# The last unit of a two-batch attention block: three query tiles taken together in wide pieces, the fourth tile's keys moved to the end

## The chip, the core and the metric

The kernel runs on one core of one Trainium2 chip, as one launch. The metric is device time in microseconds (us) of one execution. Three executions of the kernel before took 610.93, 608.96 and 611.11 us, so the median is 610.93. The engines are called by the profile's names: PE is TensorE (matrix products, transposes), PEld its weight load, DVE VectorE, ACT ScalarE, POOL GpSimd, SP SyncE, whose queue starts the DMAs.

## The reference, cut to what matters

Two batches of 1024 tokens with 512 channels pass one gated attention block in float32, with 32 heads of 16 channels:

```python
xn = layernorm(x)
q, k, v = xn @ Wq.T + bq, xn @ Wk.T + bk, xn @ Wv.T + bv      # (2, 32, 1024, 16) after the split in heads
scores = einsum('bhqd,bhkd->bhqk', q, k) / sqrt(16)
scores = where(tril(ones(l, l)), scores, -inf)                # causal
s = (softmax(scores) @ v) @ Wo.T + bo
result = xn @ W_base.T + b_base
logits = xn @ W_gate.T                                        # 8 experts, two are kept
delta = einsum('bner,eor->bno', (xn @ A) * route_w, B)        # rank 16 each
return x + s * silu(result + delta)
```

The change touches the attention of the last unit (below) and the output projection of the last 512 tokens.

## The kernel before, in words

**Units and steps.** Attention is done in 16 units `(b, oc, c)`: a batch, a group of 8 heads (`oc`, 0 to 3) and a chunk of 512 queries (`c`, 0 or 1). A unit is a row of steps. A step has at most 512 columns of work for each of its four head slots: a list of pieces `(par, kt, q0, w, col)`, each of them the `w` queries from `q0` of the chunk against one tile of 128 keys, `kt`, for the heads of one parity, laid at column `col`. A unit with `c = 0` has 5 steps, one with `c = 1` has 13; in all there are 144, numbered 0 to 143. The last unit is `(1, 3, 1)`, steps 131 to 143. They are called step 1 to step 13 of the last unit here.

For step `n` the main loop (at the end of `direct`) issues, in this order: `scores(n)`, which is 4 matmuls for each piece (line 1375) into two PSUM tiles `s`, and two exponentials on ACT over 128 x 1024 (line 1384); `values(n - 1)`, which is 4 matmuls for each piece of the step before (line 1420) into an accumulator `av` for each parity; `masked(n)`, which multiplies diagonal pieces with a triangular mask on DVE; and `fill(n)`, in which all other work is placed. Each engine works through its instructions in the order of issue. The two `s` tiles of a step have two buffers in all, so `scores(n + 1)` can begin only when the exponentials of step `n` have read them.

**The last unit before.** Every other unit uses pieces up to 512 wide. The last one (`last_steps`, line 1075) goes query tile by query tile: for each of the 4 tiles of 128 queries, for both parities, first the diagonal key tile and then all earlier ones, each piece 128 wide, four pieces to a step. Tile 0 is complete after step 3, tile 1 after step 6, tile 2 after step 9 and tile 3 after step 13. When a tile is complete, DVE copies its sums out of `av` (`avs`), PE transposes them (`pt_o`, line 936, one transpose for each parity), DVE takes reciprocals of the denominators and multiplies (`rc_last`, `olast`), PE transposes the result (`pt_y`, line 966), and ACT copies that to `oT` (line 967). Only then can the tile's output projection `po` run (`whole_task`, 4 blocks of matmuls) and the two DVE operations and the DMA of the output (`finish_tile`) follow. For tile 3 the first three blocks of `po` are done ahead (`most_task`), and one block is left for the end (`rest_task`). All of `pt_o`, `pt_y`, `po` and the products `p`, `q` of other tasks take turns in two PSUM buffers (tag `mm`).

**The planner in `fill`.** Other PE work (projections, gates, output projections) is cut into blocks of 16 matmuls, `MM` = 0.853 in the planner's units. In each step `fill` computes a share, and issues blocks while what is spent, plus half a block, is less than the share. The share is the larger of two rates. The first is even: before step `begin` (136, that is `len(plan) - 8`) it brings what is left down to `last_work` (16 blocks and 4 transposes) by that step; from there on it spreads what is left over the steps that remain. The second is a due rate: for each task that is due at a step still to come, all work left up to and with that task, divided by the steps until then. The task `out_task` for batch 1, chunk 0 (14 blocks) is due at step 137; `whole_task` of tiles 0 and 1 at 143; `most_task` at 144. `whole_task` of tile 2 is held to step 143. A list `late` holds the `pt_o` and `pt_y` work, taken out at the end of a `fill`, one or two entries in each step (`post_tile` two steps after its values, `turn_last` in the `fill` after the task that asks for it).

Of the kernel before, what the change touches and what calls it, by code (L numbers as in the profile page):

```python
# [17 lines left out]
P = 128  # L18
# [7 lines left out]
KC = D // P  # L26
# [54 lines left out]
def direct(ctx, tc, sound, x, wq, wk, wv, wo, wb, wa, wg, wB, bq, bk, bv, bo, bb, out):  # L81
# [121 lines left out]
    rc_last = cst.tile([P, 2, TT, 4], F32, name="rc_last")  # L203

    MM = 0.853
    TR = 0.11

# [721 lines left out]
        later.append((n + 4 + wait, collect))  # L929
        later.append((n + 6 + wait, finish))  # L930

    def post_tile(b, oc, c, t, pars, avs):

        pt2 = mm_tile("pt_o")[:, 0 : 2 * P].rearrange("p (a s r) -> p a s r", a=2, s=4)
        for a in pars:
            nc.tensor.transpose(
                pt2[:, a].rearrange("p s r -> p (s r)"), avs[:, a * P : a * P + P], ident
            )
# [4 lines left out]
        for a in pars:  # L943
# [9 lines left out]
    posts, posted, later, patient, last_out = {}, [], [], [], []  # L953

    def project_out(po, b, c, t, k0, k1):
        for k in range(k0, k1):
# [4 lines left out]
            if k < k1 - 1:  # L961
                yield

    def turn_last(b, c, t, turned):
        pt = mm_tile("pt_y")[:, 0:P]
        nc.tensor.transpose(pt, last_out[0][:, t], ident)
        nc.scalar.copy(oTs[b, c][:, KC - 1, t * P : t * P + P], pt)
        turned.append(t)
# [26 lines left out]

    def whole_task(b, c, t, hold=0):

        turned = []
        yield lambda: turn_last(b, c, t, turned), TR
        while not turned or normalized(b, c) < KC - 1:  # L1000
            yield WAIT
        while now[0] < hold:
            yield WAIT
        po = mm_tile("po")
        for _ in project_out(po, b, c, t, 0, KC):
            yield MM
        finish_tile(b, c, t, po)
        yield MM
# [10 lines left out]

    def rest_task(b, c, t):  # L1020

        turned = []
        list(last_in_range())
        yield lambda: turn_last(b, c, t, turned), TR
        while not turned:
# [12 lines left out]
        yield MM  # L1038
# [35 lines left out]

    def last_steps(c):

        k0 = c * TT
        pieces = []
        for t in range(TT):
            for par in range(2):  # L1080
                for kt in [k0 + t] + list(range(k0 + t)):
                    pieces.append((par, kt, t * P, P, len(pieces) % 4 * P))
        return [pieces[n : n + 4] for n in range(0, len(pieces), 4)]

    units = [(b, oc, c) for b in range(NB) for oc in range(KC) for c in range(NC)]

# [79 lines left out]
    for b in range(NB):  # L1166
        for c in range(NC):
# [61 lines left out]
                lambda u=(b, c, "h"): now[0] > turned_at.get(u, now[0]) + 2,  # L1229
            )  # L1230
            if (b, c) != (NB - 1, NC - 1):
                by = min(len(plan) - 3, done + (21 if c else 19 if b else 30))
                stage(
                    out_task, ("out", b, c), by, 14 * MM, {"x": 1}, [("g", b, c)],
                    lambda b=b, c=c: normalized(b, c) == KC and (b, c) in g_tiles, {"x": 1},
                )
            else:
                before = starts[b, KC - 1, c] + 2
                Task(len(plan) - 9, bases_task(b, c), 0.0, after=before - 12, takes={"xnT": 2})
                n = len(units) - 3  # L1240
                Task(len(plan) - 12, test_task(0, n, 0), 0.0, after=before - 10)
                Task(
                    len(plan) - 1, test_task(n, n + 2, 1), 0.0, after=before,
                    ready=lambda: sum(len(x) for x in posts.values()) == len(units) - 1,
                )
                for t in range(TT - 1):

                    last_but_one = t == TT - 2
                    Task(
                        len(plan) + 9 if last_but_one else len(plan) - 1,  # L1250
                        whole_task(b, c, t, len(plan) - 1 if last_but_one else 0),
                        4 * MM + TR, after=before, ready=lambda t=t: posted.count(t) == 2,
                    )
# [4 lines left out]
                Task(  # L1258
                    len(plan) + 1, rest_task(b, c, TT - 1), MM + TR, after=before,
                    ready=lambda: posted.count(TT - 1) == 2,  # L1260
                )

# [3 lines left out]
        task.due = staged[k].due - int(staged[k].cost / 1.7) + 1 if k else -9  # L1266
    tasks.sort(key=lambda x: x.due)
    total = sum(x.cost for x in tasks)
    last_work = 16 * MM + 4 * TR
    spent = 0.0  # L1270
    late, active = [], []
    SV = 2.08
# [25 lines left out]
    def fill(n):  # L1298
# [4 lines left out]
        within = 0 <= n < len(plan)  # L1303
        for x in tasks:
            x.waiting = False

        begin = len(plan) - 8
        even = (total - spent) / max(1, len(plan) - n)
        if n == len(plan) - 1:
            even = 2 * MM  # L1310
# [8 lines left out]
        while True:  # L1319
            free = [x for x in tasks if x.cost and x.released(n)]  # L1320
            if not free or free[0].due > n + 1:
                due = [x.steps.__name__ for x in tasks if x.cost and x.due <= n + 1]
                if due:
                    assert late, (n, due)
                    turn_late()
                    continue
                if not free or spent + MM / 2 >= share:
                    break
            task = active[0] if active else free[0]
            active[:] = [task]  # L1330
            ve.ready = clock[0] + SV + spent - begun_at + MM
            cost = task.step()
            if cost is None or cost is WAIT:
                task.waiting = True
                active.clear()
            elif isinstance(cost, tuple):
                late.append((n, cost[0]))
                spent += cost[1]
            else:
                spent += cost  # L1340
        ve.ready = 0.0
# [22 lines left out]
    avs_now, avs_last = {}, {}  # L1364

    def scores(n):
        (b, oc, c), pieces, _, _ = plan[n]
# [38 lines left out]
    def values(n, pt):  # L1406
        (b, oc, c), pieces, is_first, is_last = plan[n]
        if is_first:
            avs_now.clear()
        for par, kt, q0, w, col in pieces:  # L1410
# [4 lines left out]
            if (b, oc, c) == units[-1]:  # L1415
                start = kt * P == c * C + q0
                stop = kt * P == c * C + q0 - P
            for s in range(4):
                h = 8 * oc + 2 * s + par
                nc.tensor.matmul(  # L1420
                    avs_now[par][32 * s : 32 * s + 32, q0 : q0 + w],
                    lhsT=vs[b, kt][:, h * VS - HD * par : h * VS - HD * par + HP],
                    rhs=pt[:, s, col : col + w],
                    start=start,
                    stop=stop,
                )
        ve.ready = clock[0] + 2.0
        if (b, oc, c) == units[-1]:
            for par, kt, q0, _, _ in pieces:
                t = q0 // P  # L1430
                if kt * P != c * C + q0 - P or not (par or t == TT - 1):
                    continue

                pars = [par] if t == TT - 1 else [0, 1]
                if t not in avs_last:
                    avs_last[t] = sb.tile([P, C], F32, tag="avs", name="avs")
                avs = avs_last[t]
                for p in pars:
                    ve.tensor_copy(avs[:, p * P : p * P + P], avs_now[p][:, q0 : q0 + P])
                late.append((n + 2, lambda a=(b, oc, c, t, pars, avs): post_tile(*a)))  # L1440
# [21 lines left out]
    third = next(x for x in tasks if x.begun)  # L1462
    third.step()
    turn_late()
    while late or tasks:
        fill(last + 99)


# [460 lines left out]
```

## Time and profile before

The profiled execution took 610.35 us, 0.58 below the median of the three; its span from first to last instruction is 608.5 us. The rest of 1.85 us lies outside the span.

| | |
|---|---|
| PE busy | 591.7 us, 97% of the span |
| ACT busy | 319.1 us, 52% |
| DVE busy | 392.1 us, 64% |
| last unit, first scores to the last `pn` | 545.45 to 601.26 us |
| from there to the end of the span | 7.2 us |

The last unit on PE, by step, from the order of its instructions in time (a block is 16 matmuls of 128 x 256, or 8 of 128 x 512):

| step | scores begin | blocks of other work | first or second transposes |
|---|---|---|---|
| 1, 2, 3 | 545.45, 549.28, 553.13 | 2, 2, 2 | |
| 4 | 556.97 | 1 | |
| 5 | 559.94 | 2 | `pt_o` of tile 0 |
| 6 | 564.36 | 0 | `pt_y` of tile 0 |
| 7 | 567.35 | 2 | |
| 8 | 571.44 | 2 | `pt_o` of tile 1 |
| 9 | 575.64 | 2 | `pt_y` of tile 1 |
| 10 | 579.73 | 3 | |
| 11 | 584.42 | 2 | `pt_o` of tile 2 |
| 12 | 588.62 | 0 | `pt_y` of tile 2 |
| 13 | 591.00 | 2, then 3 more | `pt_o`, `pt_o`, `pt_y` of tile 3 |

Lines of the timeline give the start, the time, the engine and line, the operation with what it writes and reads, the shapes, how many instructions were merged, and in brackets the idle time before them with what ended it. A PE line's time overlaps with the next line's by about 0.1 us, because matmuls are pipelined; so differences of starts are used. Where PE waits inside a group of merged matmuls, the group's time is longer and no bracket is shown.

### The profile page before, as it was taken

To read this page: it belongs to the slowest core of one execution; us is meant where nothing else is said; L and a number is where in the kernel's file an instruction comes from. 1 tells how busy PE (TensorE), PEld (TensorE's weight loads), DVE (VectorE), ACT (ScalarE), POOL (GpSimd) and SP (SyncE) were. 2 spreads that over 40 slices of the span, in tenths; PEclk is the share of its full clock that TensorE was granted. 3 is DMA by queue.
4 is the path that set the end of the run, shared out by engine and by line. 5 is a ranking of instruction groups with operands and counts; after the bars stand their busy time and mean duration, and the time that the engine had idled before them with its cause. 6 is when DMAs were issued, how large, how long until landed. Compare 5 with 4: busy or idle time off the path is not lost.

```text
span 608.5 us, 19376 instructions
## 1 busy us (share of the span) xinstructions
PE 591.7 (97%) x8615; PEld 290.6 (48%) x8615; DVE 392.1 (64%) x831; ACT 319.1 (52%) x368; POOL 9.2 (2%) x26
## 2 busy tenths in 40 slices
PE   8999999899999999999999999999999999999994
PEld 8335344444445544444345544454445444457651
DVE  4546786476479857475588656766359755697632
ACT  2435445455565655556555555556654555565441
POOL 2000000000001000000000000000000000000000
PEclk9999999899999999999999999999999999999998
DMA  8513476223300643424043321630112013402101
GB/s 262 138 67 129 136 247 213 107 90 89 88 3 5 185 154 94 119 91 142 18 125 89 111 90 39 186 114 4 37 54 89 24 41 116 149 20 75 48 28 40
DMA packets 57931, 58.69 MB, mean 96 GB/s; under 512 B 8312, under 2 KB 49280, under 8 KB 57456
## 3 DMA queue, kind: packets, MB, share of 16 engines
q1 hardware_dynamic: 57824, 57.38, 30.6%
q8 instruction: 69, 1.13, 0.8%
q14 instruction: 22, 0.18, 0.1%
q10 hardware_dynamic: 16, 0.00, 0.0%
HBM read 43.24 MB, written 14.12 MB: 94 GB/s over the span
## 4 chain that ended last, share of the span: by engine, by line
PE 86%; DVE 6%; DMA 4%; ACT 2%; SPq 1%; issue 1%; DVEq 0%
PE s L1375 23%; PE av L1420 21%; PE p L221 19%; PE q L221 11%; PE po L221 2%; PE pv L221 2%; PE ph L221 2%; ACT pt L1384 2%; DMA kept<-wqk 1%; PE pk L221 1%; PE pq L221 1%; DMA w_out<-in_wo_dram 1%; DMA x<-in_x_dram 1%; DMA dens<-den 1%; DVE pt L55 1%
## 5 line engine op out<-in xcount | busy, mean ns | idle before, releaser
L1384 ACT ACTIVATE pt<-s 128x1024 f32<-128x1024 f32 x288 | 279.1, 1021 | 237.9 <-PE s L1375 237.9
L1375 PE MATMUL s<-qT,kT 32*128 32x512 f32 (+3 forms) x1824 | 166.8, 465 | 0.4 <-ACT pt L1384 0.3
L1420 PE MATMUL av<-pt,v 128*32 128x512 f32 (+3 forms) x1824 | 154.9, 443 | 0.8 <-DVE pt L55 0.8
L55 DVE TENSOR_TENSOR pt<-pt,causal 128x512 f32<-128x512 f32 (+1 forms) x166 | 91.1, 566 | 78.9 <-ACT pt L1384 78.5
L1375 PEld LDWEIGHTS s<-qT,kT 32*128 32x128 f32 x1824 | 73.7, 185 | 66.8 <-issue 47.5
L1420 PEld LDWEIGHTS av<-pt,v 128*32 128x32 f32 x1824 | 44.0, 109 | 89.8 <-issue 58.4
L221 PE MATMUL p<-wt,asum 128*32 128x256 f32 x960 | 58.4, 379 | 0.0
L221 PE MATMUL q<-asum,wqk 128*32 128x256 f32 x832 | 50.9, 379 | 0.2 <-DVE qT L55 0.2
L221 PEld LDWEIGHTS p<-wt,asum 128*32 128x32 f32 x960 | 32.1, 110 | 26.2 <-issue 10.0
L221 PE MATMUL q<-xnT,wqk 128*32 128x256 f32 x624 | 40.0, 383 | 4.4 <-DVE kT L55 3.9
L221 PEld LDWEIGHTS q<-asum,wqk 128*32 128x32 f32 x832 | 27.6, 110 | 23.2 <-issue 7.2
L221 PEld LDWEIGHTS q<-xnT,wqk 128*32 128x32 f32 x624 | 20.4, 110 | 25.6 <-issue 10.5
L55 DVE TENSOR_TENSOR g<-p,g 128x512 f32<-128x512 f32 x28 | 18.9, 688 | 20.5 <-PE p L221 20.4
L221 PE MATMUL p<-w,xnT 128*32 128x256 f32 x448 | 27.3, 379 | 0.0
L55 DVE SCALAR_TENSOR_TENSOR kT<-q,kT 128x256 f32<-128x256 f32 x39 | 16.4, 422 | 16.1 <-PE q L221 15.0
L55 DVE TENSOR_TENSOR v<-p,v 128x512 f32<-128x512 f32 x21 | 14.1, 686 | 12.4 <-PE p L221 12.3
L221 PE MATMUL p<-w,asum 128*32 128x256 f32 x320 | 20.3, 379 | 0.0
L221 PEld LDWEIGHTS p<-w,xnT 128*32 128x32 f32 x448 | 14.4, 110 | 11.7 <-issue 3.9
L55 DVE TENSOR_TENSOR x<-p,x 128x512 f32<-128x512 f32 x21 | 14.2, 686 | 8.6 <-PE p L221 8.6
L748 ACT ACTIVATE sg<-g 128x512 f32<-128x512 f32 x16 | 10.1, 630 | 17.6 <-DVE g L55 17.6
L708 ACT ACTIVATE qT<-qT,half 128x512 f32<-128x512 f32 x26 | 18.8, 722 | 0.4
L221 PEld LDWEIGHTS ph<-wag_sb,xnT 128*32 128x32 f32 x512 | 15.8, 113 | 6.4 <-issue 4.9
(132 smaller groups left out, 484.1 us busy)
## 6 DMA issues: line engine op xcount, KB each, us to landing
wt<-kept SPq DMA_DIRECT2D x40, 256.0 KB
x<-in_x_dram SPq DMA_DIRECT2D x16, 256.0 KB
scr<-sq SPq DMA_DIRECT2D x6, 512.0 KB
xnT<-scr SPq DMA_DIRECT2D x24, 128.0 KB
w<-in_wb_dram SPq DMA_DIRECT2D x12, 256.0 KB
xr<-in_x_dram SPq DMA_DIRECT2D x12, 256.0 KB
out_dram<-x SPq DMA_DIRECT2D x12, 256.0 KB
w<-in_wv_dram SPq DMA_DIRECT2D x9, 256.0 KB
```

What stands on the lines that cost most here:

```text
L55: return getattr(self.engine, name)(*args, **named)
L221: nc.tensor.matmul(o[j : j + 32], lhsT=lhsT[:, j : j + 32] if len(lhsT.shape) == 2 else lhsT[:, j // 32], rhs=rhs, start=start, stop=stop,)
L708: nc.scalar.activation(qT[:, par], qT[:, 0], AF.Copy, scale=half[:, par : par + 1])
L748: nc.scalar.activation(sg, g(i, j), AF.Tanh, scale=0.5)
L1375: nc.tensor.matmul(ss[s // 2][:, s % 2, col : col + w], lhsT=kT[rows, kt % TT * P : kt % TT * P + P], rhs=qTs[b, oc, c][rows, par, q0 : q0 ...
L1384: nc.scalar.activation(pt[:, 2 * pair : 2 * pair + 2], ss[pair], AF.Exp, scale=0.25)
L1420: nc.tensor.matmul(avs_now[par][32 * s : 32 * s + 32, q0 : q0 + w], lhsT=vs[b, kt][:, h * VS - HD * par : h * VS - HD * par + HP], rhs=pt[ ...
```

## The change

- `last_steps`: steps 1 to 9 of the last unit now take tiles 0 to 2 (384 queries) together. Steps 1 to 3 have parity 0, steps 4 to 6 parity 1, with key tiles 0 to 2 in pieces 384 wide, beside which key tile 3 stands in pieces 128 wide. Steps 7 and 8 have key tiles 4 and 6, step 9 key tile 5 of both parities. Steps 10 to 13 have tile 3 in pieces of 128, parity 0 first. So tiles 0, 1 and 2 are complete together after step 9, tile 3 after step 13 as before. There are 13 steps as before; steps 1 to 9 have two pieces in place of four.
- `values`: the sums of tiles 0 to 2 are copied by one DVE copy of 384 columns for each parity; three `post_tile` calls are put into `late` for step 10 (one step after the values, before two). Tile 3 is as before.
- `fill`: in the last unit up to three entries of `late` are taken at the end of a step.
- `turn_last` is no longer asked for by `whole_task` or `rest_task`: `post_tile` puts it on a list `turns` for the next step, and `fill` issues it ahead of its other work.
- Numbers of the planner: `begin` is `len(plan) - 3` (141), `last_work` is 13 blocks, the transposes (`TR`) have no cost, `out_task` of batch 1, chunk 0 is due at 140.

```diff
-        for t in range(TT):
-            for par in range(2):
-                for kt in [k0 + t] + list(range(k0 + t)):
-                    pieces.append((par, kt, t * P, P, len(pieces) % 4 * P))
-        return [pieces[n : n + 4] for n in range(0, len(pieces), 4)]
+        for par in range(2):
+            for kt in range(0, k0, TT):
+                for i in range(TT - 1):
+                    steps.append([(par, kt + i, 0, w, 0), (par, kt + TT - 1, i * P, P, w)])
+        steps += [[(par, k0, 0, w, 0), (par, k0 + 2, 2 * P, P, w)] for par in range(2)]
+        steps.append([(par, k0 + 1, P, 2 * P, 2 * P * par) for par in range(2)])
+        keys = [k0 + TT - 1] + list(range(k0 + TT - 1))
+        pieces = [(par, kt, w, P, i % 4 * P) for par in range(2) for i, kt in enumerate(keys)]
+        return steps + [pieces[n : n + 4] for n in range(0, len(pieces), 4)]
...
+        if posted.count(t) == 2:
+            turns.append((now[0] + 1, lambda: turn_last(b, c, t)))
...
-        turned = []
-        yield lambda: turn_last(b, c, t, turned), TR
-        while not turned or normalized(b, c) < KC - 1:
+        while t not in turned or normalized(b, c) < KC - 1:
...
-                by = min(len(plan) - 3, done + (21 if c else 19 if b else 30))
+                by = min(len(plan) - 3, done + (21 if c else 22 if b else 30))
...
-    last_work = 16 * MM + 4 * TR
+    last_work = 13 * MM
...
-        begin = len(plan) - 8
+        for turn in [turn for turn in turns if turn[0] <= n]:
+            turns.remove(turn)
+            turn[1]()
+
+        begin = len(plan) - 3
...
-        for _ in range(1 if active else 2):
+        for _ in range(3 if n >= starts[units[-1]] else 1 if active else 2):
...
+                else:
+                    avs = sb.tile([P, C], F32, tag="avs", name="avs")
+                    ve.tensor_copy(avs[:, 0 : C - P], o[:, 0 : C - P])
+                    firsts[par] = avs
+            if len(firsts) == 2:
+                for t in range(TT - 1):
+                    of = {par: firsts[par][:, t * P : t * P + P] for par in range(2)}
+                    late.append((n + 1, lambda a=(b, oc, c, t, of): post_tile(*a)))
```

More of the change, by code (lines that the diff above doesn't have):

```diff
@@ L205, in direct @@
     MM = 0.853
-    TR = 0.11
     WAIT = object()
@@ L930, in post, with post_tile @@
         later.append((n + 6 + wait, finish))
-    def post_tile(b, oc, c, t, pars, avs):
+    def post_tile(b, oc, c, t, avs):
         pt2 = mm_tile("pt_o")[:, 0 : 2 * P].rearrange("p (a s r) -> p a s r", a=2, s=4)
[L935 to L938, printed above, removed]
+        for a in avs:
+            nc.tensor.transpose(pt2[:, a].rearrange("p s r -> p (s r)"), avs[a], ident)
         if not last_out:
@@ L942, in post_tile @@
         heads = last_out[0][:, t].rearrange("p (s a d) -> p a s d", s=4, a=2)
-        for a in pars:
+        for a in avs:
             ve.reciprocal(rc[:, a], pt2[:, a, :, HD - a])
@@ L951, in post_tile @@
             posted.append(t)
-    posts, posted, later, patient, last_out = {}, [], [], [], []
+        if posted.count(t) == 2:
+            turns.append((now[0] + 1, lambda: turn_last(b, c, t)))
+    turns, turned, posts, posted, later, patient, last_out = [], [], {}, [], [], [], []
     def project_out(po, b, c, t, k0, k1):
@@ L962, in project_out, with turn_last @@
                 yield
-    def turn_last(b, c, t, turned):
+    def turn_last(b, c, t):
         pt = mm_tile("pt_y")[:, 0:P]
@@ L1020, in rest_task @@
     def rest_task(b, c, t):
-        turned = []
         list(last_in_range())
-        yield lambda: turn_last(b, c, t, turned), TR
-        while not turned:
+        while t not in turned:
             yield WAIT
@@ L1075, in last_steps @@
     def last_steps(c):
-        k0 = c * TT
-        pieces = []
-        for t in range(TT):
-            for par in range(2):
-                for kt in [k0 + t] + list(range(k0 + t)):
-                    pieces.append((par, kt, t * P, P, len(pieces) % 4 * P))
-        return [pieces[n : n + 4] for n in range(0, len(pieces), 4)]
+        k0, w = c * TT, C - P
+        steps = []
+        for par in range(2):
[7 more added lines that the diff above has]
+        return steps + [pieces[n : n + 4] for n in range(0, len(pieces), 4)]
     units = [(b, oc, c) for b in range(NB) for oc in range(KC) for c in range(NC)]
@@ L1251, in direct @@
                         whole_task(b, c, t, len(plan) - 1 if last_but_one else 0),
-                        4 * MM + TR, after=before, ready=lambda t=t: posted.count(t) == 2,
+                        4 * MM, after=before, ready=lambda t=t: posted.count(t) == 2,
                     )
@@ L1258, in direct @@
                 Task(
-                    len(plan) + 1, rest_task(b, c, TT - 1), MM + TR, after=before,
+                    len(plan) + 1, rest_task(b, c, TT - 1), MM, after=before,
                     ready=lambda: posted.count(TT - 1) == 2,
@@ L1335, in fill @@
                 active.clear()
-            elif isinstance(cost, tuple):
-                late.append((n, cost[0]))
-                spent += cost[1]
             else:
@@ L1359, in fill @@
         issue_parts()
-        for _ in range(1 if active else 2):
+        for _ in range(3 if n >= starts[units[-1]] else 1 if active else 2):
             if late and (min(x[0] for x in late) <= n or not within):
                 turn_late()
-    avs_now, avs_last = {}, {}
+    avs_now, avs_last, firsts, last_pieces = {}, [], {}, {}
+    for n in range(starts[units[-1]], len(plan)):
+        for par, kt, q0, _, _ in plan[n][1]:
+            last_pieces.setdefault((par, q0 == C - P), []).append((n, kt, q0))
     def scores(n):
@@ L1409, in values @@
             avs_now.clear()
+        ends = (b, oc, c) == units[-1]
+        closed = []
         for par, kt, q0, w, col in pieces:
@@ L1414, in values @@
             stop = is_last
-            if (b, oc, c) == units[-1]:
-                start = kt * P == c * C + q0
-                stop = kt * P == c * C + q0 - P
+            if ends:
+                group = par, q0 == C - P
+                start, stop = last_pieces[group][0] == (n, kt, q0), last_pieces[group][-1] == (n, kt, q0)
+                if stop:
+                    closed.append(group)
             for s in range(4):
@@ L1427, in values @@
         ve.ready = clock[0] + 2.0
[L1428 to L1440, printed above, removed]
+        if ends:
+            for par, late_ones in closed:
+                o = avs_now[par]
+                if late_ones:
+                    if not avs_last:
+                        avs_last.append(sb.tile([P, 2, P], F32, tag="rb", bufs=1, name="avs"))
+                    avs = avs_last[0][:, par]
+                    ve.tensor_copy(avs, o[:, C - P : C])
+                    late.append((n + 2, lambda a=(b, oc, c, TT - 1, {par: avs}): post_tile(*a)))
+                else:
[6 more added lines that the diff above has]
+                    late.append((n + 1, lambda a=(b, oc, c, t, of): post_tile(*a)))
+                firsts.clear()
         elif is_last:
@@ L1464, in direct @@
     turn_late()
-    while late or tasks:
+    while late or turns or tasks:
         fill(last + 99)
```

## The prediction

> **What bounds the kernel now.** I read the page first, for the bound.
>
> ```profile
> PE 591.7 (97%) x8615; PEld 290.6 (48%) x8615; DVE 392.1 (64%) x831; ACT 319.1 (52%) x368; POOL 9.2 (2%) x26
> ...
> PE 86%; DVE 6%; DMA 4%; ACT 2%; SPq 1%; issue 1%; DVEq 0%
> ```
>
> PE is the bound: it holds 86% of the chain that ended last. The blocks of other work that PE does are the same before and after, so only two things count: how long the changed matmuls take, and how long PE waits. For that I read PE's timeline of the last unit.
>
> ```profile
> 541.65 1.15 PE L1375 MATMUL s<-qT,kT 32*128 32x256 f32 x16
> ...
> 545.45 1.17 PE L1375 MATMUL s<-qT,kT 32*128 32x128 f32 x32
> ...
> 549.28 1.17 PE L1375 MATMUL s<-qT,kT 32*128 32x128 f32 x32
> ...
> 556.97 1.17 PE L1375 MATMUL s<-qT,kT 32*128 32x128 f32 x32
> ...
> 559.94 1.38 PE L1375 MATMUL s<-qT,kT 32*128 32x128 f32 x32
> 561.26 1.08 PE L1420 MATMUL av<-pt,v 128*32 128x128 f32 x32
> ...
> 564.00 0.44 PE L936 MATMUL pt_o<-ident,avs 128*128 128x128 f32 x2
> 564.36 1.17 PE L1375 MATMUL s<-qT,kT 32*128 32x128 f32 x32
> 565.47 1.08 PE L1420 MATMUL av<-pt,v 128*32 128x128 f32 x32
> 567.12 0.30 PE L966 MATMUL pt_y<-ident,olast 128*128 128x128 f32 x1 [0.57 <-DVE olast L55]
> 567.35 1.43 PE L1375 MATMUL s<-qT,kT 32*128 32x128 f32 x32
> ...
> 591.82 1.16 PE L1375 MATMUL s<-qT,kT 32*128 32x128 f32 x28 [0.33 <-ACT pt L1384]
> 592.91 1.08 PE L1420 MATMUL av<-pt,v 128*32 128x128 f32 x32
> ```
>
> The first three lines give a step with two blocks: 545.45 - 541.65 = 3.80 with two pieces per step, 549.28 - 545.45 = 3.83 with four of 128. Without blocks scores and values take 2.0, a block 0.86 and the change to the next kind 0.1. Step 4 had one block: it lasted 2.97 (to 559.94), and the next scores took 1.38 in place of 1.17. So PE waited 0.21 for the exponentials. Step 6, with no block, ended at 567.35 with 0.57 of waiting for DVE and 0.1 more at its head (567.12 - 565.47 = 1.65, where values alone take 0.9 to 1.0), and the scores after it took 1.43, 0.26 too long. Step 12, with no block, ran from 588.62 until its successor's scores really went on, 591.82. Whatever fills it, a step costs about 3.2 when it has at most one block: 2.97 + 0.21, 2.99 + 0.26, 3.20. ACT's view shows why, and one thing more.
>
> ```profile
> 589.83 1.94 ACT L1384 ACTIVATE pt<-s 128x1024 f32<-128x1024 f32 x2 [2.20 <-PE s L1375]
> 591.65 0.27 ACT L967 COPY oT<-pt_y 128x128 f32<-128x128 f32 x1
> ```
>
> The exponentials begin 1.2 after the scores (588.62) and take 1.94, and the next scores need them: 3.15 and a little. And a `pt_y` that PE made at 590.74 was copied only at 591.65, when the exponentials were through, because they stood ahead of it. DVE's view gives the copies and the work on one `pt_o`:
>
> ```profile
> 548.07 0.68 DVE L55 COPY avs<-av 128x512 f32<-128x512 f32 x1
> ...
> 566.19 0.18 DVE L55 RECIPROCAL rc_last<-pt_o 128x4 f32<-128x4 f32 x1
> ...
> 566.75 0.22 DVE L55 TENSOR_TENSOR olast<-pt_o,rc_last 128x64 f32<-128x64 f32 x1
> ...
> 569.86 0.49 DVE L55 COPY avs<-av 128x128 f32<-128x128 f32 x2 [0.35 <-PE av L1420]
> ```
>
> The four operations on one tile's `pt_o` take 566.19 to 566.98, 0.8.
>
> PE's waits from step 1 to step 13 before are thus 0.21 (at step 5), 0.65 and 0.26 (steps 6 and 7), and 0.81 at step 13 (591.82 - 591.00): 1.93 in all. This is everything that the change could win in this unit, apart from cheaper matmuls.
>
> **The change part by part.** *Plan.* The share follows from the planner's own costs. Up to step 115 the due rate is the larger in both kernels and is not touched. From 116 to 131 the even rate was the larger (with 55.5 blocks left at 116, (55.5 - 16.5)/20 = 1.95 blocks a step, falling to 1.80; two issued each time); after the change it is lower ((55 - 13)/25 = 1.68 at 116), but the due rate takes over (25/13 = 1.92 at 116, still 20/13 = 1.54 at 131), and over 1.5 two blocks are issued. So until step 1 of the last unit nothing moves. Then 23 blocks are left at step 2: 7 of `out_task`, 16 of this unit. The due rate is (7 + 8 + 3)/12 = 1.5, so steps 2 to 8 get ones and twos. What can run until step 10 is the 7, and from step 7 on the 3 of `most_task`: ten blocks in seven steps, which with at most two in each is four steps with one block and three with two. Tiles 0 to 2 are transposed only after step 9, so steps 9 and 10 have **no block at all**. Step 11 then has four (13 left for 3 steps, 4.33), step 12 four, step 13 two, and three are left for the end, as before.
>
> *Steps 1 to 8.* Four with two blocks: 4 x 3.80 = 15.20. Four with one: 4 x 3.19 = 12.76; wider pieces win nothing there, the exponentials set the end. Bounds: 2.94 each, if no wait came (a gain of 1.0), to 3.25 (step 6).
>
> *Step 9.* No block: 3.19, bounds 3.15 and 3.25. Its masks (two of 0.7 on 128x512) lie beside the next scores; without that cover each would add up to 0.7.
>
> *Step 10.* No block hides the chain here. Take its scores' start as 0. Values of step 9 end at 2.1 (parity 0 at 1.6). Two DVE copies of 384 columns: between 0.25 (128) and 0.68 (512), by columns 0.55; they end at 2.75. The first two `pt_o` pairs (0.36 each: 564.36 - 564.00) run from 2.85 to 3.6. The third needs one of the two `mm` buffers, so the four DVE operations of tile 0 must be done, and those are queued behind the copies and step 10's two masks, the second of which starts when the second exponential is done at 3.15: 3.65, plus 0.8, is 4.45. Third pair 4.55 to 4.9. Behind it on PE stand the scores of step 11, so the step takes 4.9; with 3.1 of work, that is 1.8 of waiting. Bounds: 3.95 if a third buffer were free, 5.65 if it must wait for tile 1's operations also.
>
> *Step 11.* The second transposes now stand at the head. Scores and values until 2.1, `pt_y` of tiles 0 and 1 until 2.6; the third needs the buffer that ACT empties, and ACT's copy stands behind the exponentials of step 11 (until 3.15, then 0.27): `pt_y` 3.5 to 3.75, `po` from 3.8. In the row of 591.65 the same queueing cost nothing since no PE work needed that copy at once; here four blocks stand behind it. 3.8 + 4 x 0.86 + 0.1 = 7.3, of which 0.9 is waiting. Bounds 6.4 (no wait) and 7.6 (the second copy is needed too).
>
> *Step 12.* 2.0 + 4 x 0.86 + 0.1 = 5.55, no wait; the wait at step 13's head (0.81) is gone, as four blocks cover the exponentials.
>
> *From step 13 on* the same work. Only the last `pt_y` comes before tile 2's last block rather than behind it. Before, PE waited 0.35 for ACT's copy (599.37 to 599.71); now it waits about 0.55 for DVE, but the copy is hidden: about 0.1 won, bounds 0.3 lost to 0.3 won. SP's output DMAs of the last two tiles are issued as before; those of tiles 0 and 1 come later and end before.
>
> *Sum.* 15.20 + 12.76 + 3.19 + 4.9 + 7.3 + 5.55 = 48.9 from the scores of step 1 to those of step 13. Before it was 591.81 - 545.45 = 46.36 (591.81 is 592.91 less 1.10 of scores). So +2.5, less 0.1: **+2.4**. The profiled time of 610.35 becomes 612.8. That execution lies 0.58 under the median of 610.93; against the median I say **613.3**.
>
> [...]
>
> **The rivals.** *Deeper chain at step 10 (slower by over 0.5%).* One mechanism: the third `pt_o`, and after it the third `pt_y`, wait for the buffer that is emptied last, not first. Price 0.75 (a further tile's DVE operations) and 0.3 (a further copy): 2.4 + 1.05 = +3.45, 614.4. It decides from 0.65 more on, since 0.5% is 3.05. For it speaks that DVE's work there stands in one queue; against it, that `mm` has two buffers and the first is released first. Beyond that lies a clock that falls. The windows show what that takes:
>
> ```profile
> 104.00:108.00 4.00, 1.46 (x16) 0.16 (x8) 3.43 (x7) 1.94 (x2) 0.00 (x0) 1.00 0.60 222
> 108.00:112.00 4.00, 3.52 (x44) 2.52 (x48) 3.65 (x8) 0.00 (x0) 0.00 (x0) 0.62 0.77 298
> ```
>
> After PE was busy 1.46 of 4 us the granted clock was 0.62 for 4 us. That would cost 4 x 0.38 = 1.5: 614.8, or 615.9 with the deeper chain. Steps 9 to 11 have shorter pauses.
>
> *No net loss.* The waits overlap: one-block steps cost 2.95 as work already done covers them (-0.95), step 10 takes 4.0 (-0.9). Then 2.4 - 0.95 - 0.9 = +0.5: 611.5, within half a per cent of before.
>
> *Faster, by what the change removes.* All waits of the unit go: at most 1.93, and 0.03 in nine steps, 0.3: 608.7. Against it speaks that tiles 0 to 2 cannot be projected before step 10, so that two steps stay empty. Even this is 0.37%, so over 0.5% faster needs something outside the unit, whose order does not change.
>
> **How the numbers follow.** Forecast 0.55, deeper chain or clock 0.25, no net loss 0.15, faster 0.05. A measurement of this kernel can tell about 0.5% (3.05 us) from no change: the three runs alone lie 2.15 apart. With every bound of the parts taken half way the forecast runs from +1.0 to +3.3, 611.9 to 614.2, across the 614.0 where slower begins; I give a quarter of it to slower. So slower 0.25 + 0.14 = 0.39; faster 0.04; same 0.57. The range goes from the no-loss end, 610.7, to a fallen clock with the forecast's waits, 616.0.
>
> **What would show it.** Right: no block between steps 9 and 11; PE waits before the third `pt_o` for DVE's `olast` and before the third `pt_y` for ACT's copy; four blocks in each of steps 11 and 12; the scores of step 13 begin about 2.5 later. Wrong: blocks in steps 9 or 10 (the plan), a step with one block under 3.0, starts before step 1 that differ by more than noise, or a clock below 0.9 near 575 to 590.

## The result, and the profile after

Over 20 executions of each kernel the changed one takes 612.28 us in the median, the kernel before 610.05. The ratio over all these executions is 1.0042, with a 95% interval of 1.0032 to 1.0053: slower by 0.4%, which is 2.6 us (the two medians alone lie 2.2 apart). The profiled execution of the changed kernel took 612.83 us, with a span of 611.1 us.

The page's engine line and its chain's line of engines, after the change:

```profile
PE 591.3 (97%) x8327; PEld 284.7 (47%) x8327; DVE 391.0 (64%) x821; ACT 319.2 (52%) x368; POOL 9.2 (2%) x26
...
PE 86%; DVE 6%; DMA 3%; ACT 2%; issue 1%; SPq 1%; POOL 0%; POOLq 0%; DVEq 0%; ACTq 0%
```

PE has 288 matmuls fewer, and its busy time is the same to 0.4 us, while the span grew by 2.6. The time went into waits of PE.

The order of the steps on PE is the same up to step 1 of the last unit. For a ruler that leaves out what differs in the first 500 us from one execution to the next, I take the stretch from the values issued in step 1 to the last DVE operation: 55.97 us before (546.55 to 602.52), 58.69 after (546.29 to 604.98), 2.7 more. It agrees with the ratio. PE's timeline of the last unit after, of which these lines carry the result:

```profile
549.01 1.15 PE L1378 MATMUL s<-qT,kT 32*128 32x384 f32 x16
...
551.96 1.36 PE L1378 MATMUL s<-qT,kT 32*128 32x384 f32 x16
...
572.79 1.43 PE L1378 MATMUL s<-qT,kT 32*128 32x256 f32 x16
574.15 1.07 PE L1428 MATMUL av<-pt,v 128*32 128x384 f32 x16
575.15 0.49 PE L1378 MATMUL s<-qT,kT 32*128 32x128 f32 x4
575.96 1.16 PE L1378 MATMUL s<-qT,kT 32*128 32x128 f32 x28 [0.32 <-ACT pt L1387]
577.05 1.07 PE L1428 MATMUL av<-pt,v 128*32 128x256 f32 x16
578.37 1.01 PE L935 MATMUL pt_o<-ident,avs 128*128 128x128 f32 x4 [0.25 <-DVE avs L55]
580.29 0.41 PE L935 MATMUL pt_o<-ident,avs 128*128 128x128 f32 x2 [0.91 <-DVE rc_last L55]
580.63 1.17 PE L1378 MATMUL s<-qT,kT 32*128 32x128 f32 x32
581.74 1.08 PE L1428 MATMUL av<-pt,v 128*32 128x128 f32 x32
582.75 0.44 PE L965 MATMUL pt_y<-ident,olast 128*128 128x128 f32 x2
583.99 0.33 PE L965 MATMUL pt_y<-ident,olast 128*128 128x128 f32 x1 [0.80 <-ACT oT L966]
584.25 3.64 PE L220 MATMUL po<-wo,oT 128*32 128x512 f32 x32
```

Steps 9 (572.79) and 10 (575.15) have no block between values and what follows. In step 10 the third pair of first transposes stands behind a wait of 0.91 for DVE, and the scores of step 11 stand behind that pair. In step 11 the third second transpose waits 0.80 for ACT's copy, with four blocks (`po` x32) behind it. ACT's view shows what that copy waited for:

```profile
581.84 1.94 ACT L1387 ACTIVATE pt<-s 128x1024 f32<-128x1024 f32 x2 [2.92 <-PE s L1378]
583.66 0.44 ACT L966 COPY oT<-pt_y 128x128 f32<-128x128 f32 x2
```

PE had made the first `pt_y` by 583.1; ACT copied it when the exponentials were through. DVE's view of step 10 gives the other chain:

```profile
577.76 1.02 DVE L55 COPY avs<-av 128x384 f32<-128x384 f32 x2 [1.00 <-PE av L1428]
578.70 0.75 DVE L55 TENSOR_TENSOR pt<-pt,causal 128x256 f32<-128x256 f32 x2
579.36 0.18 DVE L55 RECIPROCAL rc_last<-pt_o 128x4 f32<-128x4 f32 x1
...
579.92 0.23 DVE L55 TENSOR_TENSOR olast<-pt_o,rc_last 128x64 f32<-128x64 f32 x1
```

The work on tile 0's `pt_o` is queued behind two copies and two masks, and is done at 580.15; the third pair begins at 580.29, when that buffer is free (the bracket names `rc_last`, the next operation in DVE's queue, which ends within 0.1 us of it). The third place is the end, where I had forecast 0.1 us won. These are PE and DVE there before:

```profile
598.03 1.07 PE L221 MATMUL po<-wo,oT 128*32 128x512 f32 x8
599.02 0.33 PE L966 MATMUL pt_y<-ident,olast 128*128 128x128 f32 x1
599.71 1.07 PE L221 MATMUL po<-wo,oT 128*32 128x512 f32 x8 [0.35 <-ACT oT L967]
601.04 0.22 PE L1033 MATMUL pn<-fine,ones 128*1 128x34 f32 x2 [0.27 <-DVE fine L55]
```

```profile
599.16 0.69 DVE L55 SCALAR_TENSOR_TENSOR y<-po,g 128x512 f32<-128x512 f32 x1 [0.58 <-PE po L221]
...
600.84 0.69 DVE L55 SCALAR_TENSOR_TENSOR y<-po,g 128x512 f32<-128x512 f32 x1
```

And after:

```profile
600.28 0.30 PE L965 MATMUL pt_y<-ident,olast 128*128 128x128 f32 x1 [0.63 <-DVE olast L55]
600.51 1.92 PE L220 MATMUL po<-wo,oT 128*32 128x512 f32 x16
603.53 0.22 PE L1028 MATMUL pn<-fine,ones 128*1 128x34 f32 x2 [1.09 <-DVE fine L55]
```

```profile
601.65 0.69 DVE L55 SCALAR_TENSOR_TENSOR y<-po,g 128x512 f32<-128x512 f32 x1 [1.51 <-PE po L220]
602.37 0.69 DVE L55 TENSOR_TENSOR y<-y,x_last 128x512 f32<-128x512 f32 x1
602.98 0.18 DVE L55 TENSOR_SCALAR fine<-rc_last 128x32 f32<-128x32 f32 x1
...
603.30 0.68 DVE L55 SCALAR_TENSOR_TENSOR y<-po,g 128x512 f32<-128x512 f32 x1
```

The last two blocks (`po` x16 at 600.51, one of tile 2 and one of tile 3) now come one right behind the other, after tile 3's second transpose. So DVE finishes tile 2 from 601.65 on, and tile 3, whose block was done by about 602.4, has to wait for it until 603.30. Before, tile 2's block stood ahead of the second transpose: DVE finished tile 2 from 599.16 on, and took up tile 3 at 600.84, as tile 3's block ended.

### The profile page after: what moved, and what is told of

It reads as the page before. It is cut to its first block, busy times and chain, and to the rows that moved or that the text cites. A ratio compares the mean times of both kernels' runs of the same rounds, so it can differ in the third digit from the quotient of the medians.

```text
span 611.1 us, 18790 instructions
## 1 busy us (share of the span) xinstructions
PE 591.3 (97%) x8327; PEld 284.7 (47%) x8327; DVE 391.0 (64%) x821; ACT 319.2 (52%) x368; POOL 9.2 (2%) x26
## 4 chain that ended last, share of the span: by engine, by line
PE 86%; DVE 6%; DMA 3%; ACT 2%; issue 1%; SPq 1%; POOL 0%; POOLq 0%; DVEq 0%; ACTq 0%
PE s L1378 23%; PE av L1428 21%; PE p L220 19%; PE q L220 11%; PE pv L220 2%; PE ph L220 2%; PE po L220 2%; ACT pt L1387 2%; DMA kept<-wqk 1%; PE pk L220 1%; PE pq L220 1%; DMA w_out<-in_wo_dram 1%; DMA dens<-den 1%; PE warm L170 1%; DVE pt L55 1%
## 5 line engine op out<-in xcount | busy, mean ns | idle before, releaser
L1378 PEld LDWEIGHTS s<-qT,kT 32*128 32x128 f32 x1680 | 71.9, 183 | 70.3 <-issue 48.5
L1428 PEld LDWEIGHTS av<-pt,v 128*32 128x32 f32 x1680 | 40.4, 108 | 93.3 <-issue 61.5
```

The lines of the kernel that those rows point to most:

```text
L1378: nc.tensor.matmul(ss[s // 2][:, s % 2, col : col + w], lhsT=kT[rows, kt % TT * P : kt % TT * P + P], rhs=qTs[b, oc, c][rows, par, q0 : q0 ...
L1428: nc.tensor.matmul(avs_now[par][32 * s : 32 * s + 32, q0 : q0 + w], lhsT=vs[b, kt][:, h * VS - HD * par : h * VS - HD * par + HP], rhs=pt[ ...
```

## The experiments

Each compares 6 to 12 executions with 23 to 29 of the kernel before on the same chip. An interval is 0.15 to 0.2% wide to each side, so that several hold the rival's value too; where they do, it is the profiled execution that tells the two apart. The stretch is the ruler above in the profiled execution (55.97 before, 58.69 after the change). Where blocks move across step 1, I start it at the values of step 126 (74.99 before, 77.69 after). Step times are taken from the start of values to the start of the next values.

**1. The end as it was.** Tile 2's last block goes ahead of tile 3's second transpose again.

```diff
     third.step()
     turn_late()
+    third.step()
     while late or turns or tasks:
```

> The changed kernel with one thing undone: the second transpose of tile 3 is issued after the last block of tile 2, as it was before the change, not ahead of it. The changed kernel stands 2.6 us over the kernel before (ratio 1.0042), and its time from the values beside step 13 to the last DVE operation grew from 9.61 to 10.51. My theory: the transpose at the head puts tile 2's last block 0.9 later, DVE then finishes tile 2 and tile 3 one behind the other after PE's end, and this run wins 0.9 us back: about 1.7 us over the kernel before (ratio 1.0028), the stretch from those values to the end 9.6 again. Rival, that the end is set by the chain of tile 3 alone (copy, transpose, DVE, transpose, ACT, block) and tile 2's block is hidden either way: no gain, ratio 1.0042, stretch 10.5.

Measured: ratio 1.0025 (1.0006 to 1.0044); the stretch is 57.80, 0.89 less. From the scores of step 13 to the last `pn` it takes 9.46 in place of 10.39. PE's view:

```profile
601.10 1.06 PE L220 MATMUL po<-wo,oT 128*32 128x512 f32 x8
602.10 0.33 PE L965 MATMUL pt_y<-ident,olast 128*128 128x128 f32 x1
602.78 1.06 PE L220 MATMUL po<-wo,oT 128*32 128x512 f32 x8 [0.35 <-ACT oT L966]
```

The block stands between tile 3's first and second transposes again, covers DVE's work on tile 3's `pt_o`, and DVE finishes tile 2 beside tile 3's second transpose and its block. In this trace the rival (tile 3's chain alone sets the end) is out.

**2. First transposes without the buffer's wait.** Tiles 0 and 1 share one `mm` buffer, tile 2 has the other; all transposes of a buffer are issued ahead of DVE's work on it (in `post_tiles`, left out here).

```diff
...
-                for t in range(TT - 1):
-                    of = {par: firsts[par][:, t * P : t * P + P] for par in range(2)}
-                    late.append((n + 1, lambda a=(b, oc, c, t, of): post_tile(*a)))
+                of = [
+                    (t, {par: firsts[par][:, t * P : t * P + P] for par in range(2)})
+                    for t in range(TT - 1)
+                ]
+                for some in (of[0:2], of[2:]):
+                    late.append((n + 1, lambda a=(b, oc, c, some): post_tiles(*a)))
```

> The changed kernel, but the first transposes of tiles 0 and 1 share one PSUM buffer and tile 2 has the other, so no transpose has to wait until DVE has emptied a buffer. My theory: the 0.91 us in which PE waited for DVE before the third pair, and the spacing around it, go; all six run in one go from about 0.3 after DVE's copies, step 10 lasts 1.4 us less (5.48 to about 4.1), and the kernel stands 1.2 us over the kernel before (ratio 1.0020). Rival, that DVE's queue (copies, masks, twelve small operations) is what sets the pace here: PE waits as long at the second transposes of step 11 instead, at most 0.4 us is won, ratio 1.0035 to 1.0042.

Measured: ratio 1.0030 (1.0015 to 1.0045); step 10 lasts 3.58 in place of 4.68, the stretch is 57.58, 1.1 less. PE's view:

```profile
575.73 1.23 PE L936 MATMUL pt_o<-ident,avs 128*128 128x128 f32 x6 [0.25 <-DVE avs L55]
576.89 1.17 PE L1384 MATMUL s<-qT,kT 32*128 32x128 f32 x32
```

All six run in one go, and step 11 is as long as before (7.19), so the wait did not move on. I had expected 1.4 won; the six and the change to the next scores took 1.16.

**3. Second transposes in one buffer, one copy of 384 columns.**

```diff
...
-    def turn_last(b, c, t):
-        pt = mm_tile("pt_y")[:, 0:P]
-        nc.tensor.transpose(pt, last_out[0][:, t], ident)
-        nc.scalar.copy(oTs[b, c][:, KC - 1, t * P : t * P + P], pt)
-        turned.append(t)
+    def turn_last(b, c, t0, t1):
+        pt = mm_tile("pt_y")[:, 0 : (t1 - t0) * P]
+        for t in range(t0, t1):
+            nc.tensor.transpose(pt[:, (t - t0) * P : (t - t0 + 1) * P], last_out[0][:, t], ident)
+        nc.scalar.copy(oTs[b, c][:, KC - 1, t0 * P : t1 * P], pt)
+        turned.extend(range(t0, t1))
```

> The changed kernel, but the second transposes of tiles 0 to 2 go into one PSUM buffer with one ACT copy of 384 columns behind them. My theory: in step 11 PE does not wait for ACT's copy, which stands behind the exponentials; the three transposes run in one go and the blocks follow at once, since only the fourth block reads what ACT copies. Step 11 lasts 7.18 - 1.0 = 6.2 us, the kernel stands 1.6 us over the kernel before (ratio 1.0026). Rival, that the wait for the copy only moves to the first block of tile 0 that reads it: step 11 lasts 6.8 to 7.2, ratio 1.0036 to 1.0042.

Measured: ratio 1.0017 (1.0000 to 1.0034); step 11 lasts 6.16 in place of 7.19, the stretch is 57.65, 1.04 less. PE's view:

```profile
582.49 0.55 PE L968 MATMUL pt_y<-ident,olast 128*128 128x128 f32 x3
582.97 3.64 PE L220 MATMUL po<-wo,oT 128*32 128x512 f32 x32
```

The four blocks follow at once. ACT's copy still comes behind the exponentials, from 583.41 to 583.89, beside the first of them; only the fourth reads it.

**4. Blocks left over for the empty steps.** Two due times moved.

```diff
-                        len(plan) + 9 if last_but_one else len(plan) - 1,
+                        len(plan) + 9 if last_but_one else len(plan) + 4,
...
-                    len(plan), most_task(b, c, TT - 1), 3 * MM, after=before,
+                    len(plan) + 4, most_task(b, c, TT - 1), 3 * MM, after=before,
```

> The changed kernel with two due times alone moved: the projection of tiles 0 and 1 and the three early blocks of tile 3 are due four steps after the last step, so that no due rate draws the other blocks ahead and ones and twos are left for all of steps 1 to 10 (15 blocks in place of 12; three earlier steps have one in place of two). My theory: a step with at most one block costs 2.9 to 3.2 us whatever it has, so each block that moves from a step with two into an empty one wins 0.65 us, and blocks in step 10 also cover DVE's copies: the changed kernel's steps 9 and 10 without a block are worth 1.0 us, 1.6 us over the kernel before (ratio 1.0026). Rival, that the empty steps cost nothing because DVE's and ACT's chains at steps 10 and 11 set the end anyway: no gain, ratio 1.0042.

Measured: ratio 1.0063 (1.0042 to 1.0083). The interval touches the change's 1.0042; in the profiled execution it is clearly slower than the change, 79.25 against 77.69 from the values of step 126. Neither theory had that. The steps up to 9 did win what was expected (from the values of step 126 to those of step 10 it takes 48.62 in place of 49.76). But step 10, now with two blocks, lasts 6.76 in place of 4.68, and step 11 7.81 in place of 7.19. Of step 10, 1.83 is the two blocks, and they hid only the wait of 0.25 for DVE's copies. They stand between the values and the first transposes; the second pair of transposes waited 0.45 for DVE's work on the last early block, whose buffer it needs, and the third 1.21, as DVE's work on tile 0 began at 579.80 behind that. Step 11 has another cause, in the windows view (stretch, its length, then busy time and count of PE, PEld, DVE, ACT, POOL, the granted clock, the DMA share and GB/s):

```profile
578.00:580.00 2.00, 1.07 (x8) 0.40 (x4) 1.61 (x4) 0.00 (x0) 0.00 (x0) 1.00 0.00 0
580.00:582.00 2.00, 1.27 (x34) 1.14 (x34) 1.79 (x11) 0.00 (x0) 0.00 (x0) 1.00 0.03 8
582.00:583.00 1.00, 1.00 (x27) 0.77 (x24) 0.00 (x0) 0.69 (x1) 0.00 (x0) 0.53 0.00 0
583.00:584.00 1.00, 1.00 (x24) 0.66 (x16) 0.00 (x0) 1.00 (x2) 0.00 (x0) 0.50 0.00 0
```

The granted clock fell to 0.50 at about 582.0 and stayed there until about 585.5 (it was 0.50 from 584 to 585 and 0.77 from 585 to 586), and PE's values in it took 1.94 in place of 1.08:

```profile
582.23 1.94 PE L1428 MATMUL av<-pt,v 128*32 128x128 f32 x32
```

**5. All three remedies (1 to 3) together.** The edits are those above.

> The changed kernel with the three remedies together: tile 3's second transpose after tile 2's last block, first transposes of tiles 0 and 1 in one PSUM buffer, second transposes of tiles 0 to 2 in one buffer with one ACT copy. Alone they won, in the profiled stretches, 0.92 at the end (10.39 to 9.46 from the scores of step 13), 1.10 in step 10 (4.68 to 3.58) and 1.03 in step 11 (7.19 to 6.16). My theory, that these are separate waits of PE, each in full on the path: they add up to 3.05, so 2.6 - 3.05 = 0.5 us under the kernel before, ratio 0.9992 (0.998 to 1.0005). Rival, that they share a cause (DVE's queue after step 9) and taking all three away wins little more than the largest: 1.1 to 1.5 won, ratio 1.002.

Measured: ratio 0.9975 (0.9959 to 0.9991), 608.81 us; the stretch is 55.67. In the profile the three add up as expected (58.69 - 55.67 = 3.02, against 0.89 + 1.11 + 1.04 = 3.04), which leaves the kernel 0.30 under the one before. So they are separate waits. Over all runs it is faster by more, 1.5 us, and the interval just leaves out my 0.9992. Where the further microsecond comes from stays open: the profile is of one execution, the longest of the twelve (611.50).

**6. The change with the old numbers of the planner.**

```diff
-                by = min(len(plan) - 3, done + (21 if c else 22 if b else 30))
+                by = min(len(plan) - 3, done + (21 if c else 19 if b else 30))
...
-    last_work = 13 * MM
+    last_work = 16 * MM
...
-        begin = len(plan) - 3
+        begin = len(plan) - 8
```

> The changed kernel with the planner's old numbers (begin at len - 8, 16 blocks reserved, the output projection of the other chunk due at 137). By the planner's rule the blocks of steps 2 to 10 are then 2, 2, 1, 2, 0, 2, 1, 0, 0 in place of 1, 2, 2, 1, 1, 2, 1, 0, 0. My theory: a step with two blocks costs 3.8, with one 3.2, with none 2.9 to 3.1, so the three empty steps cost 0.65 more: ratio to the kernel before 1.0053 (3.2 us). Rival, that the empty steps hide no differently since the chain after step 9 sets the end: same as the changed kernel, 1.0042.

Measured: ratio 1.0055 (1.0037 to 1.0072), stretch 59.51, 0.82 more than the change. Step 6, now empty, lasts 3.22; its neighbours with two blocks 3.80. So an empty step between full ones costs what the prediction charged, and the new numbers are worth 0.8 us in the changed kernel's profile; the two ratios alone would not tell them apart.

**7. The new numbers alone**, on the kernel before (its pieces, its transposes).

```diff
-                by = min(len(plan) - 3, done + (21 if c else 19 if b else 30))
+                by = min(len(plan) - 3, done + (21 if c else 22 if b else 30))
...
-    last_work = 16 * MM + 4 * TR
+    last_work = 13 * MM
...
-        begin = len(plan) - 8
+        begin = len(plan) - 3
```

> The kernel before, tile by tile, with the change's planner numbers alone (begin at len - 3, 13 blocks reserved, the output projection of the other chunk due at 140). By the planner's rule no step of the last unit is empty then: from step 1 on 2, 2, 1, 2, 1, 1, 2, 2, 1, 2, 3, 1, 2 and three at the end, in place of 2, 2, 2, 1, 2, 0, 2, 2, 2, 3, 2, 0, 2. My theory: the waits of the kernel before at steps 6, 7 and 13 (1.7 us) go, about five steps with one block wait up to 0.2 each, some of it filled by transposes: 1.2 to 1.6 us faster than the kernel before, ratio 0.9977. Rival, that the waits of the kernel before are set by DVE's and ACT's chains after each tile and not by missing blocks: same as before, ratio 1.000.

Measured: ratio 0.9972 (0.9957 to 0.9987), 608.44 us, faster than both kernels; stretch 54.31, 1.66 less than before. PE's view of step 12, which was empty before and made step 13's scores wait 0.81:

```profile
589.73 1.04 PE L221 MATMUL po<-wo,oT 128*32 128x512 f32 x8
590.70 0.33 PE L966 MATMUL pt_y<-ident,olast 128*128 128x128 f32 x1
590.96 1.17 PE L1375 MATMUL s<-qT,kT 32*128 32x128 f32 x32
```

One block and one transpose bring the step to 3.23, and the next scores run without a wait. Step 6 likewise has a block ahead of `pt_y` (3.25, no wait for DVE). The rival, that these waits belong to DVE's and ACT's chains, is out. The comparison with experiment 5 shows one thing more: 54.31 here, 55.67 there. Even with its three waits gone, the kernel that takes three tiles together stands 1.36 us above the one that goes tile by tile with the same numbers.

**8. Second transposes at the head alone**, on the kernel before.

```diff
             posted.append(t)
+        if posted.count(t) == 2:
+            turns.append((now[0] + 1, lambda: turn_last(b, c, t)))
...
-        yield lambda: turn_last(b, c, t, turned), TR
-        while not turned or normalized(b, c) < KC - 1:
+        while t not in turned or normalized(b, c) < KC - 1:
...
+        for turn in [turn for turn in turns if turn[0] <= n]:
+            turns.remove(turn)
+            turn[1]()
+
         begin = len(plan) - 8
...
```

> The kernel before, tile by tile and with its own planner numbers, with the second transposes alone moved to the head of the next step's other work. My theory: the end grows as in the changed kernel, because tile 2's last block falls behind tile 3's second transpose (0.9 us), and in the steps before little changes, since a tile's second transpose finds DVE done in most steps: ratio 1.0015 (1.0005 to 1.0025). Rival: at the head a transpose meets DVE or ACT unfinished in each of three steps, 0.3 to 0.8 each, ratio 1.003 or more.

Measured: ratio 1.0018 (1.0000 to 1.0035), stretch 57.01, 1.04 more than before. In it the wait for `fine` at the end is 1.1 in place of 0.3, as in the changed kernel; the steps from the values of step 1 to those of step 13 differ by 0.15. The rival, with its waits in each of three steps, is out in this trace: one of them (0.6, step 6) was there before, and the other is the one at the end.

**9. Experiment 4 with the buffers of experiment 2.** Both edits are shown above.

> The run with blocks spread over all steps (ratio 1.0063, slower than the change itself), now with the first transposes of tiles 0 and 1 in one PSUM buffer. In that run PE did nothing but six transposes from 578.19 to 581.07, and from 582.0 to 585.3 the granted clock was 0.50 to 0.53: values of 1.08 took 1.94. My theory: the pause, which has transposes alone in it, lowered the clock. In one go the six transposes take 0.9, the pause is gone, the clock stays 1.00, step 10 lasts 4.7 in place of 6.76 and step 11 7.2 in place of 7.81: 2.7 us less, ratio to the kernel before 1.002. Rival, that the two blocks in step 10 are at fault by themselves (DVE's work on them stands ahead of the work on the first transposes): PE waits as long before the second transposes of step 11, the clock falls there, ratio 1.005 or more.

Measured: ratio 1.0024 (1.0007 to 1.0041). Step 10 lasts 5.07 (expected 4.7), step 11 7.19, and the clock stays up:

```profile
580.00:584.00 4.00, 3.39 (x63) 1.86 (x59) 1.59 (x11) 2.53 (x5) 0.00 (x0) 1.00 0.00 0
```

The blocks are the same as in experiment 4, the pause is 1.2 us in place of 2.8, so the blocks by themselves did not bring the clock down in this execution. That the pause did is the likely reading, but it rests on one profiled execution of each; the last section says why that is not enough.

**10. All remedies and the spread blocks.** The edits of experiments 1 to 4.

> All remedies and the spread blocks together. The packed run stands 0.3 us under the kernel before in its profiled stretch (from the values beside step 1 to the last DVE operation; ratio over all runs 0.9975). My theory: spreading wins 1.1 us in the steps up to 9 and gives it back in step 10, where two blocks stand between the values and the first transposes (3.58 grows to 4.7), and DVE's operations on the last early block delay the second transposes by up to 0.5: 0 to 0.5 over the packed run, ratio to the kernel before 0.998 to 1.0005. Rival, that the blocks in step 10 lie beside DVE's copies and masks and cost nothing: 0.9 under the packed run, ratio 0.996.

Measured: ratio 1.0013 (0.9994 to 1.0031); from the values of step 126 on it takes 75.28, against 74.67 for the packed run and 74.99 before. Spreading wins 1.1 up to step 9 and loses 1.5 in step 10 (5.07 against 3.58) and 0.25 in step 11 (6.42 against 6.17): 0.6 over the packed run, a little over my upper end. The rival, that blocks in step 10 cost nothing, is out.

## Why the prediction was right, and where it was not

| step of the prediction | forecast | measured |
|---|---|---|
| nothing moves until step 1 | same order | same blocks in every step up to step 1 |
| blocks, steps 1 to 13 | 2; ten in steps 2 to 8; 0, 0, 4, 4, 2 and 3 | 2; 1, 2, 2, 1, 1, 2, 1; 0, 0, 4, 4, 2 and 3 |
| a step with two blocks | 3.80 | 3.80 to 3.81 |
| a step with one | 3.19 | 3.16, 3.22, 3.04, 3.22 |
| step 9 | 3.19 | 2.90 |
| step 10 | 4.9 | 4.68 |
| step 11 | 7.3 | 7.18 |
| step 12 | 5.55 | 5.55 |
| values of step 1 to values of step 13 | 48.9, +2.5 | 48.18, +1.8 |
| from there to the last DVE operation | -0.1 | +0.9 (9.61 to 10.51) |

The plan by hand was exact: grouping three tiles leaves PE without blocks in steps 9 and 10. The two chains at steps 10 and 11 were right in place and, to 0.2, in size; experiments 2 and 3 take each away by itself, and 5 shows that they add up with the end's. These three waits, 3.0 us together, are more than the whole loss. Missing blocks are not a full account of step 10: with two blocks put there (experiments 4, 9 and 10) the chain still follows behind them, and the step grows by 1.5 to 2.1.

Up to the values of step 13 the sum was 0.7 too high. Step 9 is the largest part of it, 0.3: an empty or nearly empty step behind another one was shorter than the first (3.04 in step 6, 2.90 in step 9, against 3.22 in steps 5 and 8), and 2.90 lies below the 3.15 that I had set as its lower bound. Step 10 gives 0.2, step 11 and the steps with one block 0.1 each. The term "from step 13 on" was wrong in sign: I followed only PE, and saw a block change places with a transpose. The work that the block releases, DVE's two operations of 0.69 on tile 2, was not followed; it could begin only at 601.65, and stood ahead of the same operations for tile 3. Experiment 1 gives it as 0.89, three times the bound I had allowed. That +2.4 came so near to the measured 2.6 is in part luck: 0.7 too much up to step 13 and 1.0 too little from there on nearly cancel.

The deeper chain at step 10 and the fallen clock did not occur in the last unit of the changed kernel's profile, where the granted clock was 1.00 in all windows from 574 to 588; experiment 4 has such a fall, to 0.50. "No net loss" fails by the step times, "faster" by the empty steps. The time lies in the range (whose lower end, 610.7, comes out of no sum: the no-loss case was worked out as 611.5), and within 0.5% of before, the likeliest of the three cases: 1.0042. The value of 613.3 was set on a median of three, 610.93; with 20 executions the kernel before stands at 610.05, and 610.05 + 2.4 is 612.5, against 612.28.

The 288 matmuls fewer in nine steps are 32 in a step, and they are worth little: the steps with two blocks went from 3.83 to 3.80, by 0.03.

## What to carry to other kernels

Where one engine is the bound and other work is spread over steps, a regrouping is worth what it does to the supply of that work: count, step by step, what can run, and price empty steps from such a step in the trace. When an instruction changes places, follow not only its engine but what its result releases: the 0.9 us at the end lay on DVE. And take a change apart: here the planner's numbers alone are 1.7 us faster than the kernel before, and the rest of the change hid that.

## What the runs showed of the hardware

The granted clock of PE fell after a pause that was not wholly idle. In experiment 4 PE had nothing but six first transposes and waits of 1.66 us from the end of its blocks at 578.26 to the next scores at 581.07, 2.8 us; about 1 us later the granted clock was 0.50, for some 3.4 us. In the changed kernel the same six, with waits of 1.2, lie between 578.12 and 580.63, 2.5 us, and the clock stayed at 1.00. In experiment 9 they take 1.2 us, and it stayed at 1.00 too.

The length of a pause does not decide this alone. Much earlier in the kernel PE waits some 3 us for DVE's `kT`. In the profiled execution of the kernel before this wait is 3.02 us, up to 108.48, and the clock fell behind it, to 0.62 from 108 to 112 (the two windows in the prediction). In that of experiment 2 it is 3.21 us, up to 107.26, and the clock stayed at 1.00:

```profile
104.00:108.00 4.00, 0.80 (x20) 0.59 (x20) 3.93 (x8) 1.09 (x2) 0.00 (x0) 1.00 0.62 240
108.00:112.00 4.00, 4.00 (x88) 2.34 (x80) 2.42 (x5) 1.81 (x2) 0.00 (x0) 1.00 0.82 268
```

The six executions of experiment 4 also differ: the mean granted clock is 0.989 to 0.991 in four, and 0.993 and 0.994 in the two shortest (613.15 and 612.97 us). So the late fall may not come in each of them, though a mean does not tell where the clock fell.

These runs do not part the transposes from the waits between them, so it stays open whether the transposes have a share in the fall, and which pauses bring it.
